# Walking the moving operand and the PSUM output of split matmuls from the last column to the first

## Chip, cores and metric

The kernel runs on one core of one Trainium2 chip. The metric is the device time of one execution in microseconds, as the median of several runs.

## What is computed

The reference is one block of a perceiver with a latent `x` of 256 tokens by 512 features and a context of 25088 tokens by 512 features: a cross attention with a sigmoid in place of the softmax, a causal self attention with compressed keys and values, and a mixture of eight experts with one expert per token. Nearly all of the arithmetic is in the cross attention, which cut to what matters is:

```python
qp = layernorm(x) @ Wq.T + bq            # 256 x 128
kp = ctx @ Wk.T + bk                     # 25088 x 128
vp = ctx @ Wv.T + bv                     # 25088 x 512
z  = sigmoid(qp @ kp.T / sqrt(128))      # 256 x 25088
x  = x + z @ vp
x  = x + attn(layernorm(x))              # causal, 16 heads, rotary part
x  = x + ffn(layernorm(x))               # argmax over 8 experts, relu(g)^2 * u
```

All inputs are fp32.

## The kernel before

An fp32 product is made of three matmuls in a 4-byte format of TensorE that the program calls fp32r. Each operand is split into a high part (the value copied to fp32r) and a low part (the value less its high part). The helper `split` does that: ScalarE copies (line 64), VectorE subtracts (line 65). The helper `mm3` then issues three matmuls into one PSUM tile: high by high (line 68), high by low (line 69), low by high (line 70). `ahi` and `alo` are the stationary operand, loaded into the array ahead of each matmul; `bhi` and `blo` are the moving operand, whose columns are streamed through it; `ps` is the output in PSUM, one column for each moving column.

The value projection is not applied to the context: since `z @ (ctx @ Wv.T)` is `(z @ ctx) @ Wv.T`, the kernel accumulates `z @ ctx` over all keys and applies `Wv` once at the end.

The context is worked off in 49 chunks of 512 keys. It is loaded twice from HBM in two layouts, features first (`rT`) and keys first (`rN`), each 1 MB per chunk, on SyncE's queue, two to three chunks ahead. For one chunk the loop does the following:

- `kp_mm`: four calls of `mm3` over blocks of 128 features, with `wk` stationary and the split `T` moving, 512 columns, into the tile `kp_ps`; `kp_out` adds the bias and splits the result.
- `scores`: twice per chunk, two calls of `mm3` each, with 128 keys of `kp` stationary and `qp` moving, 256 columns, into the two halves of one PSUM bank, the tile `sc`; then the sigmoid (`z`), its sum over keys (`zacc`) and its split.
- `av`: eight calls of `mm3` per chunk, with `z` stationary and the split `N` moving, 512 columns, into `acc`, two PSUM banks that stay open over all chunks.

Besides, `prepare` splits the weights of the experts and of the last projection a piece at a time and spills them to HBM.

After the loop come the value projection (`V`, tile `v_ps`), the self attention, whose matmuls are mostly plain fp32 ones outside `mm3` (the scores `S` at line 428, among others), its output projection (`WO`, tile `wo_ps`), and the experts (`GU`, tile `gu`, 256 columns, and `DN`, tile `fo`, 512 columns). `V`, `WO`, `GU` and `DN` go through `mm3` too, and so does the projection of the queries (`qp_ps`, 256 columns) at the start.

The order on each engine is the order in which the program is written: the function `in_order` ties every instruction of TensorE, ScalarE, VectorE and GpSimd to the one before it on its engine. Waits between engines come from the tiles that they share.

Of the kernel before, what the change touches and what calls it, by code (L numbers as in the profile page):

```python
# [48 lines left out]
def body(ctx, tc, a, out, nch=NCH):  # L49
# [15 lines left out]
        eng.tensor_tensor(lo, src, f(hi), ALU.subtract)  # L65

    def mm3(ps, ahi, alo, bhi, blo, first, last):
        mm(ps, lhsT=ahi, rhs=bhi, start=first, stop=False)  # L68
        mm(ps, lhsT=ahi, rhs=blo, start=False, stop=False)  # L69
        mm(ps, lhsT=alo, rhs=bhi, start=False, stop=last)  # L70
# [4 lines left out]
    def bank(name):  # L75
        return psum.tile([P, D], F32, tag="b", name=name, bufs=6)
# [91 lines left out]
    def kp_mm(c, blocks=range(KD)):  # L168
        th, tl = sT[c]
        if c not in kp:  # L170
            kp[c] = bank(f"kp_ps{c}")
        ps = kp[c]
        for j in blocks:
            mm3(ps, wk[0][:, toks(j)], wk[1][:, toks(j)], th[:, j, :], tl[:, j, :], j == 0, j == KD - 1)
# [6 lines left out]
    def scores(c, p):  # L181
        ps = bank(f"sc{c}_{p}").rearrange("p (i t) -> p i t", i=2)
        for i in range(2):
            t = toks(2 * p + i)
            mm3(ps[:, i, :], kp[c][0][:, t], kp[c][1][:, t], qp[0], qp[1], True, True)
        z = sb.tile([P, 2, T], F32, tag="z", name=f"z{c}_{p}", bufs=2)
        nc.scalar.activation(z, ps, AF.Sigmoid, scale=1.0 / math.sqrt(128.0))  # L187
        zz[c, p] = pair(f"z{c}_{p}", [P, 2, T], "z", 2 * LAG)
        tt2(zacc, zacc, z, ALU.add)  # L189
        split(*zz[c, p], z)  # L190

    def av(c, t, q):
        zh, zl = zz[c, t // 2]
        nh, nl = sN[c]
        mm3(acc[q], zh[:, t % 2, toks(q)], zl[:, t % 2, toks(q)], nh[:, t, :], nl[:, t, :],
            c == 0 and t == 0, c == nch - 1 and t == NT - 1)
# [48 lines left out]
    ps = bank("qp_ps")[:, :T]  # L245
# [319 lines left out]
    ps = bank("rows_ps")  # L565
# [205 lines left out]
```

## Time and profile before

| | us |
|---|---|
| median of 3 runs (lowest to highest) | 586.33 (585.92 to 586.8) |
| the profiled execution's own time | 586.28 |
| its span, first to last instruction | 584.5 |
| TensorE busy | 570.6 |
| VectorE busy | 459.7 |
| ScalarE busy | 395.1 |
| mean granted TensorE clock | 1.0 |

A profile is of one execution. In it, PE is TensorE's matmuls, PEld its loads of the stationary operand, DVE is VectorE, ACT is ScalarE, POOL is GpSimd and SP is SyncE. A line of the groups gives the code line, the engine, the operation, the tiles (output <- inputs), the shape and the count, then the busy time in us and the mean of one instruction in ns, then the idle time of the engine just before. In the 40 slices each digit is a share in tenths. The chain of waits is followed back from the last instruction to whatever released it; in order of time each of its pieces is given with its start, its length and its engine, tile and line. Matmuls are pipelined, and the ends of their records are modelled, so their starts say more than their lengths.

### The profile page before, as it was taken

What the parts mean: (1) busy time and instruction counts of PE and PEld (TensorE: products, weight loads), DVE (VectorE), ACT (ScalarE), POOL (GpSimd) and SP (SyncE); (2) the same over time, 40 slices, a digit from 0 to 9 for tenths busy, and PEclk for the clock granted to TensorE, in tenths of its full rate; (3) what the DMA queues carried; (4) which work ended last, traced back from release to release, by engine and by line L of the source; (5) the groups of instructions that cost most, each with busy time, mean ns of one, the idle gap of its engine ahead of it and who ended that gap; (6) DMA issues with size and microseconds to landing.
All of it is one profiled execution on the core that took longest, in us unless ns stands there. A gap on an engine that the chain in (4) does not pass through costs nothing.

```text
span 584.5 us, 8061 instructions
## 1 busy us (share of the span) xinstructions
PE 570.6 (98%) x3036; PEld 481.7 (82%) x3036; DVE 459.7 (79%) x528; ACT 395.1 (68%) x512; POOL 21.1 (4%) x28
## 2 busy tenths in 40 slices
PE   4999999999999999999999999999999999999997
PEld 3888888888888888888888888888888887876996
DVE  6898888888888888888888888787878765667543
ACT  5877777777777777777777776767676752574211
POOL 5200000000000000000000000000000041000000
PEclk9999999999999999999999999999999999999999
DMA  8897887879888888788988887565657477700000
GB/s 288 334 368 283 278 295 281 321 278 317 287 324 276 325 271 325 266 337 298 332 282 319 274 337 245 208 225 206 234 198 243 149 295 262 316 1 1 1 1 36
DMA packets 33526, 144.94 MB, mean 248 GB/s; under 512 B 4240, under 2 KB 4432, under 8 KB 19792
## 3 DMA queue, kind: packets, MB, share of 16 engines
q1 hardware_dynamic: 33488, 144.44, 69.3%
q8 instruction: 23, 0.38, 0.2%
q14 instruction: 15, 0.12, 0.1%
HBM read 129.22 MB, written 15.20 MB: 247 GB/s over the span
## 4 chain that ended last, share of the span: by engine, by line
PE 95%; DVE 3%; DMA 1%; issue 0%; POOL 0%; ACT 0%; SPq 0%; POOLq 0%
PE acc L68 15%; PE acc L69 15%; PE acc L70 15%; PE kp_ps L70 8%; PE kp_ps L69 8%; PE kp_ps L68 8%; PE sc L70 4%; PE sc L69 4%; PE sc L68 4%; PE s L428 2%; PE gu L68 1%; PE gu L69 1%; PE gu L70 1%; PE pt L445 1%; DMA wq_r<-in_wq 1%; PE pv L456 1%
## 5 line engine op out<-in xcount | busy, mean ns | idle before, releaser
L68 PE MATMUL acc<-N,z 128*128 128x512 f32 x392 | 153.9, 393 | 0.0
L69 PE MATMUL acc<-N,z 128*128 128x512 f32 x392 | 153.7, 392 | 0.0
L65 DVE TENSOR_TENSOR N<-rN,N 128x2048 fp32r<-128x2048 f32 (+1 forms) x53 | 111.6, 2110 | 52.3 <-ACT N L64 52.2
L70 PE MATMUL acc<-N,z 128*128 128x512 f32 x392 | 152.5, 389 | 0.0
L65 DVE TENSOR_TENSOR T<-rT,T 128x2048 fp32r<-128x2048 f32 (+1 forms) x49 | 110.3, 2252 | 15.3 <-ACT T L64 15.3
L187 ACT ACTIVATE z<-sc 128x512 f32<-128x512 f32 x98 | 58.7, 599 | 66.5 <-PE sc L70 66.2
L64 ACT CAST N<-rN 128x2048 fp32r<-128x2048 f32 (+1 forms) x55 | 94.4, 1725 | 6.1
L64 ACT CAST T<-rT 128x2048 fp32r<-128x2048 f32 (+1 forms) x55 | 94.3, 1721 | 0.9 <-DMA rT<-in_ctxT 0.7
L70 PEld LDWEIGHTS acc<-N,z 128*128 128x128 f32 x392 | 73.6, 188 | 16.0
L68 PEld LDWEIGHTS acc<-N,z 128*128 128x128 f32 x392 | 74.0, 189 | 12.3
L69 PEld LDWEIGHTS acc<-N,z 128*128 128x128 f32 x392 | 74.0, 189 | 11.7
L68 PE MATMUL kp_ps<-T,wk 128*128 128x512 f32 x196 | 76.9, 392 | 0.0
L70 PE MATMUL kp_ps<-T,wk 128*128 128x512 f32 x196 | 76.7, 392 | 0.0
L69 PE MATMUL kp_ps<-T,wk 128*128 128x512 f32 x192 | 74.7, 389 | 0.0
L189 DVE TENSOR_TENSOR zacc<-zacc,z 128x512 f32<-128x512 f32 x98 | 67.2, 686 | 3.7 <-ACT z L187 1.7
L65 DVE TENSOR_TENSOR z<-z,z 128x512 fp32r<-128x512 f32 x98 | 67.3, 686 | 0.0
L64 ACT CAST z<-z 128x512 fp32r<-128x512 f32 x98 | 61.0, 623 | 3.1
L178 ACT ACTIVATE kp<-kp_ps,bk 128x512 fp32r<-128x512 f32 x49 | 33.9, 691 | 39.9 <-PE kp_ps L70 39.9
L70 PE MATMUL sc<-qp,kp 128*128 128x256 f32 x196 | 55.8, 285 | 0.1
L69 PE MATMUL sc<-qp,kp 128*128 128x256 f32 x196 | 55.4, 283 | 0.0
L68 PE MATMUL sc<-qp,kp 128*128 128x256 f32 x196 | 54.9, 280 | 0.0
L68 PEld LDWEIGHTS kp_ps<-T,wk 128*128 128x128 f32 x196 | 37.1, 189 | 7.8
(177 smaller groups left out, 658.5 us busy)
## 6 DMA issues: line engine op xcount, KB each, us to landing
rN<-in_ctxN SPq DMA_DIRECT2D x49, 1024.0 KB, 5.7
rT<-in_ctxT SPq DMA_DIRECT2D x47, 1024.0 KB, 5.5
sp_gu<-w_gu SPq DMA_DIRECT2D x32, 256.0 KB, 4.3
gu<-sp_gu SPq DMA_DIRECT2D x8, 1024.0 KB, 6.0
r_gu<-in_gu SPq DMA_DIRECT2D x16, 256.0 KB, 5.7
sp_dn<-w_dn SPq DMA_DIRECT2D x16, 256.0 KB, 4.3
dn<-sp_dn SPq DMA_DIRECT2D x16, 256.0 KB, 6.0
r_dn<-in_dn SPq DMA_DIRECT2D x8, 256.0 KB, 6.1
```

Of the source, the lines that this page charges most:

```text
L64: copy(hi, src)
L65: eng.tensor_tensor(lo, src, f(hi), ALU.subtract)
L68: mm(ps, lhsT=ahi, rhs=bhi, start=first, stop=False)
L69: mm(ps, lhsT=ahi, rhs=blo, start=False, stop=False)
L70: mm(ps, lhsT=alo, rhs=bhi, start=False, stop=last)
L178: nc.scalar.activation(kp[c][0], ps, AF.Identity, bias=bk)
L187: nc.scalar.activation(z, ps, AF.Sigmoid, scale=1.0 / math.sqrt(128.0))
L189: tt2(zacc, zacc, z, ALU.add)
L428: mm(p3[:, h - h0:h - h0 + 2, :], lhsT=qs[:, tt, h // 2, g, :], rhs=kbd[g // 2][:, g % 2, h:h + 2, :nk], start=tt == 1, stop=tt == 0 and h ...
L445: nc.tensor.transpose(ps[:, toks(i * (tt + 1) + kt)], pr[tt, u][:, i, toks(kt)], ident)
L456: mm(pv[tt][r, g, :], lhsT=vs[kt][:, g * P + r.start:g * P + r.stop], rhs=pt[tt, u][:, toks(i * (tt + 1) + kt)], start=kt == 0, stop=kt == tt)
```

## The change

`mm3` reverses the column axis of its PSUM output and of both moving operands ahead of its three matmuls. The column that was streamed first is now streamed last, and is written to the same place in PSUM as before. The stationary operands are left as they are, and so are all matmuls outside `mm3`.

```diff
     def mm3(ps, ahi, alo, bhi, blo, first, last):
+
+        ps, bhi, blo = ps[:, ::-1], bhi[:, ::-1], blo[:, ::-1]
         mm(ps, lhsT=ahi, rhs=bhi, start=first, stop=False)
         mm(ps, lhsT=ahi, rhs=blo, start=False, stop=False)
         mm(ps, lhsT=alo, rhs=bhi, start=False, stop=last)
```

The three matmuls stand on lines 70 to 72 of the changed file, and everything below them two lines further down.

## Prediction

> **What bounds the kernel now.** I read the page's first two parts, then the chain of waits, then the instruction groups.
>
> ```profile
> PE 570.6 (98%) x3036; PEld 481.7 (82%) x3036; DVE 459.7 (79%) x528; ACT 395.1 (68%) x512; POOL 21.1 (4%) x28
> PE   4999999999999999999999999999999999999997
> PEclk9999999999999999999999999999999999999999
> PE 95%; DVE 3%; DMA 1%; issue 0%; POOL 0%; ACT 0%; SPq 0%; POOLq 0%
> ```
>
> The reader is to see that TensorE works in all 40 slices at the full granted clock, and that 95% of the chain that ended last is TensorE. "Busy" alone proves little for a pipelined engine; the chain does, because it stays on the engine and names no wait. The groups say which matmuls:
>
> ```profile
> L68 PE MATMUL acc<-N,z 128*128 128x512 f32 x392 | 153.9, 393 | 0.0
> L68 PE MATMUL kp_ps<-T,wk 128*128 128x512 f32 x196 | 76.9, 392 | 0.0
> L68 PE MATMUL sc<-qp,kp 128*128 128x256 f32 x196 | 54.9, 280 | 0.0
> ```
>
> Lines 68, 69 and 70 are the three matmuls of mm3, and the three tiles have such rows for each. The 392 ns is a record from start to modelled end and overlaps the next. What a matmul costs is the distance to the next start, and the chain, in order of time, gives that:
>
> ```profile
> 298.30 0.23 PE kp_ps L68
> ...
> 303.74 0.12 PE sc L68
> ...
> 304.45 0.23 PE acc L68
> ...
> 305.84 0.12 PE sc L68
> ```
>
> From 298.30 to 303.74 lie 24 matmuls of 512 columns: 227 ns each. From 303.74 to 304.45, six of 256 columns: 118 ns. From 304.45 to 305.84, six of 512: 232 ns; the acc stream mixes 227 and 232, and I take 229. Doubling the columns from 256 to 512 adds 109 ns, so a matmul costs some 0.43 ns a column and about 10 ns fixed. The stage is set by columns.
>
> The same view shows what half that rate looks like, in two places:
>
> ```profile
> 10.68 0.43 PE kp_ps L68
> 11.11 0.43 PE kp_ps L69
> ...
> 13.24 0.21 PE qp_ps L68
> ...
> 521.33 0.86 PE s L428 x2
> ```
>
> The first matmuls of the run, the same instructions as later, take 427 ns (10.68 to 13.24, six) and the first qp ones 213 ns. The plain fp32 matmuls of the scores take 430 ns for 512 columns. In both, the fixed cost is nearly gone beside the doubled column time.
>
> **What the Trainium skill says.** (1) "Advanced Engine Details and Errata", PSUM Cachelines: 8-byte lines, two fp32 values; "Any non-contiguous AP significantly slows down matmuls"; every two consecutive elements should be contiguous. No row before has a step other than one in the innermost dimension, so the trace neither agrees nor disagrees. (2) "SBUF — State Buffer", A bandwidth-pool intuition that's wrong, note on cachelines: 16-byte lines, full bandwidth needs two hits in a line. A walk by minus one has four fp32 hits in each line, and two in each PSUM line: read by the letter this lets the reversed walk go free. (3) "TensorE: Matmul & The Clock Gate", Back-to-back issue gap: N/1.2 ns cold and N/2.4 + 2.5 ns warm. The trace agrees on the first (427 and 213 ns); of the second it shows 227 and 118, about 11 ns over, where the page has 216 and 109. (4) "Advanced Engine Details and Errata", 2x-1p Requirements: VectorE's packed mode takes a step of +1 or -1. That is another engine, a hint only that -1 can count as contiguous.
>
> **The change part by part.** No instruction, DMA, wait or tile is added, removed or moved. The reversed operands cover the same bytes, so each split, each copy out of PSUM and each DMA waits for the same matmul as before; a reader waits for the end of a whole matmul, so that column 0 is now written last makes nobody later. SP's and POOL's queues are not touched. The stationary operand keeps its walk, and so do the matmuls outside mm3 (plain fp32, transposes, masks). Slicing is done while the program is built and costs no device time.
>
> What is left is the rate at which 2652 matmuls stream: acc 1176, kp 588, sc 588, gu 192, qp 12, fo 48, v and wo 24 each, counted in the groups. Nothing before shows a reversed stream, so it is bounded from both sides:
> - At best the walk is free: 0. Slightly better cannot be excluded, because I cannot say what the 11 ns over the page's gap are made of.
> - At worst in the likely class, two consecutive columns no longer merge into one access, and the stream falls to one column where it had two. The price of that is in the rows above: 427 to 430 ns for 512 columns, 213 to 215 for 256. I take 428 and 214.
>
> The sum at half rate:
> - kp: 588 x (428 - 227) = 118 us
> - acc: 1176 x (428 - 229) = 234 us
> - sc: 588 x (214 - 118) = 56 us
> - gu and qp: 204 x 96 = 20 us
> - v, wo, fo: 96 x (428 - 230) = 19 us
>
> Together 447 us. The twelve matmuls at the start of the run that already go at 427 and 213 ns come off (6 x 0.20 + 6 x 0.10 = 1.8 us). TensorE idles 13.9 us in all (584.5 - 570.6), most of it before its first matmul and around the last copies, which a longer stream cannot fill; I take off 2 us more for the gaps that it can. That leaves 443 us, all on the path: TensorE is the bound and becomes more so. VectorE's 459.7 us and ScalarE's 395.1 us of work would fall to 45% and 38% of the span, and their waits for sc and kp would grow without costing anything; the DMA, 0.85 busy in the windows of the main loop, would fall to about half that.
>
> The profiled execution took 586.28 us with a span of 584.5, so 1.8 us lie around the span; the median of the runs, 586.33, is the same within 0.05. The half-rate case gives 584.5 + 443 + 1.8 = 1029 us.
>
> I choose half rate as the likeliest, over free: the skill's sentence on PSUM names a direct slowdown of matmuls, the merging of two fp32 columns into one 8-byte line has to hold on the write side and on the moving side at once, and either failing is enough. [...]
>
> **The rivals.**
> - **The walk is free** (also if the build folds the two reversals away: reversing both sides permutes columns and leaves each product where it was, so nothing of the work depends on it). For it: two consecutive columns stay in one line whichever way they are walked, and both ends are aligned, since each slice starts at a multiple of 256 columns. Against it: the skill's "any". Time: 586 us, change 0.
> - **A fixed price per matmul.** The stream keeps its rate but its start or its turn at the end costs some cycles more. Each nanosecond on 2652 matmuls is 2.7 us; 1 to 10 ns give 589 to 613 us. Nothing in the profile speaks for it except that a fixed cost of about 11 ns exists.
> - **Faster.** That fixed cost belongs to the warm three-pass matmul: bf16 mask matmuls of 512 columns start the next after 0.21 us in the timeline (504.93 to 505.14) where these take 227 ns. If it comes from the order in which a matmul's first columns meet what the one before left in flight, the reversed order could remove it: 2652 x 10.5 ns = 28 us, giving 558 us. It decides from 0.45 ns a matmul (1.2 us in all). Against it: all three passes are reversed together, so consecutive matmuls meet each other as before, end against start.
> - **Worse than half rate.** One element at a time on both sides with no overlap, or a fall to a quarter: some 850 ns for 512 columns and 425 for 256. On 1860 and 792 matmuls that adds 1860 x 0.62 + 792 x 0.31 = 1399 us: about 1980 us. Only the word "significantly" speaks for it.
>
> **How the numbers follow.** A measurement of this kernel can tell about 0.2%, 1.2 us, from no change. Half rate: 0.50, 1029 us. Its own range is 1015 to 1066: the low end if the waits in the prologue and tail absorb 14 us, the high end if the fixed cost of 11 to 13 ns stays on top of the doubled columns (2652 x 0.012 = 32 us, with a little for the spread of the acc starts). Free: 0.20. A fixed price per matmul: 0.12. Worse than half rate: 0.06. Faster: 0.12. Slower is then 0.50 + 0.12 + 0.06 = 0.68, within the bound 0.20, faster 0.12. Cases of more than one sign hold real chance, so the range that holds 8 in 10 runs from the free case (585) to the top of half rate (1066); it leaves out the faster case and the quarter rate, 0.18. The middle of that range is nearly empty: it is wide because the price of a reversed stream is unknown before, in one step.
>
> **What would show it right or wrong.** Right: in the chain of the changed kernel kp_ps and acc pieces of 0.43 us and sc pieces of 0.21 us where there were 0.23 and 0.12, the granted clock still 1.0, TensorE's share of the chain at 97% or more, VectorE near 45% and ScalarE near 38% busy, with the same number and length of their instructions; the L428 pieces, which mm3 does not touch, still 0.86 for two. The first six kp_ps matmuls of the run would stay at 0.43: if these too double, the rate is lost per array cycle, and the loss is more than the merging of two columns. Free would show 0.23 and 0.12 everywhere. A fixed price would show the same nanoseconds added at 256 and at 512 columns. What makes the prediction wrong in kind is a matmul that keeps its start-to-start of 227 ns; what makes it wrong in size is a doubled one off 428.

## The result, and the profile after

| | before | changed |
|---|---|---|
| median, us | 586.57 (585.92 to 587.5, 4 runs) | 595.04 (594.31 to 595.31, 4 runs) |
| profiled execution: its time, its span | 586.28, 584.5 | 595.31, 593.5 |

The changed kernel is slower by 8.5 us: ratio 1.0141, 95% interval 1.0124 to 1.0159. The sign was forecast; the size, 1029 us, was not.

The page of the changed kernel, its busy times, TensorE's two rows of slices, and the chain by engine:

```profile
PE 580.0 (98%) x3036; PEld 481.8 (81%) x3036; DVE 459.7 (77%) x528; ACT 394.1 (66%) x512; POOL 21.1 (4%) x28
PE   4999999999999999999999999999999998999997
PEclk9999999999999999999999999999999999999999
PE 97%; DVE 1%; POOL 1%; DMA 0%; issue 0%; ACT 0%; POOLq 0%
```

TensorE was the bound and still is, at the same granted clock. VectorE's work is the same to 0.1 us. The groups of mm3, one row for each tile:

```profile
L70 PE MATMUL acc<-N,z 128*128 128x512 f32 x392 | 155.7, 397 | 0.0
L70 PE MATMUL kp_ps<-T,wk 128*128 128x512 f32 x196 | 78.5, 400 | 0.0
L70 PE MATMUL sc<-qp,kp 128*128 128x256 f32 x196 | 55.3, 282 | 0.0
```

The mean records at 512 columns are 4 to 8 ns longer than before (393 and 392), those at 256 columns 2 ns (280). The chain in order of time, one chunk of the loop. A piece of a matmul starts there where the record before it ends, some 160 ns after the matmul's own start; over a whole run of equal matmuls the distance from piece to piece is that from start to start:

```profile
303.50 0.23 PE kp_ps L70
...
306.30 0.23 PE acc L70
...
309.10 0.12 PE sc L70
...
309.81 0.23 PE acc L70
...
311.21 0.12 PE sc L70
```

The pieces are printed as 0.23 and 0.12 as before; only distances over several of them show the change. Twelve kp matmuls take 2.80 us, 233 ns each, where they took 227; twelve of acc likewise 2.80 us. Six of sc take 0.71 us, 118 ns, as before. The six of acc behind them take 1.40 us, 233 ns each, where they took 232.

Means over all starts between 40 and 440 us of the two traces: kp 226.7 to 233.3 ns, acc 228.9 to 233.3, sc 118.8 to 118.9. The sum closes: 588 x 6.6 ns = 3.9 us and 1176 x 4.4 ns = 5.2 us make 9.1 us. The stretch from the first kp matmul to the last of acc grew from 482.3 to 491.5 us, by 9.2; the rest of the span is 0.3 us shorter at the start and within 0.1 us behind the loop. So the change is a longer start-to-start distance of the 512-column matmuls of the loop, 2 to 3% of it. It is no chance collision with other engines or with DMA: matmul by matmul, the distances of some 40 like chunks agree within 1 ns in each of the two kernels.

The two places that I had named as a sign:

```profile
10.37 0.43 PE kp_ps L70
...
12.93 0.21 PE qp_ps L70
...
531.20 0.86 PE s L430 x2
```

At the start of the run the reversed matmuls still take 427 ns (10.37 to 12.93, six): no price is seen there. The matmuls outside mm3 keep their 430 ns.

### The profile page after: what moved, and what is told of

It is laid out like the page before. It is cut to its first block, busy times and chain, and to the rows that moved or that the text cites. A ratio compares the mean times of both kernels' runs of the same rounds, so it can differ in the third digit from the quotient of the medians.

```text
span 593.5 us, 8111 instructions
## 1 busy us (share of the span) xinstructions
PE 580.0 (98%) x3036; PEld 481.8 (81%) x3036; DVE 459.7 (77%) x528; ACT 394.1 (66%) x512; POOL 21.1 (4%) x28
## 4 chain that ended last, share of the span: by engine, by line
PE 97%; DVE 1%; POOL 1%; DMA 0%; issue 0%; ACT 0%; POOLq 0%
PE acc L71 15%; PE acc L70 15%; PE acc L72 15%; PE kp_ps L71 8%; PE kp_ps L70 8%; PE kp_ps L72 8%; PE sc L72 4%; PE sc L71 4%; PE sc L70 4%; PE s L430 2%; PE gu L70 1%; PE gu L72 1%; PE gu L71 1%; PE q_ps L356 1%; PE pt L447 1%; PE pv L458 1%
## 5 line engine op out<-in xcount | busy, mean ns | idle before, releaser
L71 PE MATMUL acc<-N,z 128*128 128x512 f32 x392 | 156.0, 398 | 0.0
L70 PE MATMUL acc<-N,z 128*128 128x512 f32 x392 | 155.7, 397 | 0.0
L72 PE MATMUL acc<-N,z 128*128 128x512 f32 x392 | 155.5, 397 | 0.0
L71 PEld LDWEIGHTS acc<-N,z 128*128 128x128 f32 x392 | 73.7, 188 | 13.3
L70 PE MATMUL kp_ps<-T,wk 128*128 128x512 f32 x196 | 78.5, 400 | 0.0
L72 PE MATMUL kp_ps<-T,wk 128*128 128x512 f32 x196 | 78.3, 400 | 0.0
L71 PE MATMUL kp_ps<-T,wk 128*128 128x512 f32 x192 | 76.3, 397 | 0.0
```

## The experiments

Four questions: which side pays, which property of the walk, how it goes with length and with the neighbouring matmuls, and whether any use of it is a gain. Where an edit is said to be for 512 columns only, it stands under `if ps.shape[-1] == 512`.

### Which side pays

```diff
 def mm3(ps, ahi, alo, bhi, blo, first, last):
+    bhi, blo = bhi[:, ::-1], blo[:, ::-1]
```

> Only the moving operands of mm3 are reversed; the PSUM outputs are walked forward, so every mm3 product has its columns in reversed order (the work is the same, the values are not the reference's). In the changed kernel every mm3 matmul of 512 columns starts the next after 233 ns instead of 227 (kp and the first half of acc) or 231 (the second half of acc), while those of 256 columns stay at 118 to 119 ns. Theory A, the price sits on the read of the moving operand: 233 ns here too, about 595 us (+8.5 us). Theory B, it sits on the write to PSUM: 227 ns and 586.5 us, no change. Theory C, each side pays half: about 230 ns, 590 to 591 us.

Measured: 595.44 us, ratio 1.0158 (1.0142 to 1.0174).

```diff
 def mm3(ps, ahi, alo, bhi, blo, first, last):
+    ps = ps[:, ::-1]
```

> Only the PSUM outputs of mm3 are reversed; the moving operands are walked forward (again the columns of every mm3 product stand in reversed order). Theory A, read of the moving operand: 227 ns for 512 columns of kp, 586.5 us. Theory B, write to PSUM: 233 ns, about 595 us. Theory C, half each: 230 ns, 590 to 591 us. If both this and the run with the moving operand alone give 233 ns, the two prices run side by side and are not added.

Measured: 586.05 us, ratio 0.9998 (0.999 to 1.0007). The chain in order of time of the first, then of the second:

```profile
303.80 0.23 PE kp_ps L69
...
306.60 0.23 PE acc L69
```

```profile
306.86 0.23 PE kp_ps L69
...
309.58 0.23 PE acc L69
```

Twelve kp matmuls take 2.80 us with the moving operand reversed and 2.72 us with the output reversed: 233 against 227 ns. Theory A holds. The read of the moving operand pays all of it; a PSUM output written from the last column to the first is free, in accumulating matmuls too. With one side reversed alone, the build cannot have folded the reversal away, since the columns land in another order.

### Which matmuls pay

```diff
+    if ps.shape[-1] == 512:
+        ps, bhi, blo = ps[:, ::-1], bhi[:, ::-1], blo[:, ::-1]
```

> Both sides reversed, but only in the mm3 matmuls of 512 columns (kp, acc, v, wo, fo: 1860 of 2652). If the 256-column matmuls hide the price behind the load of their weights (their 118 ns is that load's pace, not the columns'), all of the change is here: 595 us, with 233 ns for kp and acc. If the price is on every matmul and the 256-column ones pay it too, about 592 us (8.5 us less 792 of 2652).

Measured: 595.7 us, ratio 1.0165 (1.0146 to 1.0184), kp at 233.3 ns and acc at 233.7. All of the change is in the 512-column matmuls.

```diff
+    if ps.shape[-1] == 256:
+        ps, bhi, blo = ps[:, ::-1], bhi[:, ::-1], blo[:, ::-1]
```

> Both sides reversed only in the mm3 matmuls of 256 columns (sc, gu, qp: 792 of 2652). Hidden behind the weight load: 586.5 us within 0.5, sc at 118.8 ns in the mean. A fixed price on every matmul: 792 x 6.7 ns = 5.3 us more, 592 us. If instead the second half of acc, which follows sc and runs at 231 ns before, is set by the state that sc leaves the pipe in, acc's times there may move although its own walk is forward.

Measured: 584.07 us, ratio 0.9967 (0.9956 to 0.9979): no price, but a gain of 2.1 us. It is taken up again below.

### Which property of the walk

Four walks that cover the same columns, on both sides, for 512 columns only. `t` is each of ps, bhi and blo.

```diff
+    t.rearrange("p (a b) -> p a b", b=4)[:, :, ::-1]     # inner4
```

> 512-column mm3 only: the columns are walked in groups of four fp32 (16 bytes) from the first group to the last, but inside each group from the last to the first, on moving operand and output alike. Theory order inside a line: the price comes from taking a group's elements backwards, 233 ns or more. Theory descending addresses: groups ascend here, so 227 ns and 586 us. If a walk with two steps costs by itself, both this and the next run are above 233 ns.

Measured: 585.88 us, ratio 0.9999 (0.9989 to 1.0009), kp at 226.7 ns.

```diff
+    t.rearrange("p (a b) -> p a b", b=4)[:, ::-1, :]     # lines4
```

> 512-column mm3 only: groups of four fp32 walked from the last group to the first, inside each group forward. Theory descending addresses, or the start at the far end of the row: 233 ns, about 595 us. Theory order inside a line: 227 ns, 586 us.

Measured: 595.93 us, ratio 1.0171 (1.0132 to 1.0211), kp at 233.3 ns.

```diff
+    t.rearrange("p (a b) -> p a b", b=256)[:, ::-1, :]   # halves
```

> 512-column mm3 only: columns 256 to 511 are walked first and then 0 to 255, each half forward, on both sides. Theory start at the far part of the row: 233 ns, 595 us. Theory descending addresses: only one backward jump, 227 ns, 586 us.

Measured: 585.75 us, ratio 0.999 (0.998 to 1.0), kp at 226.7 ns.

```diff
+    t.rearrange("p (a b) -> p a b", b=256)[:, :, ::-1]   # halves_rev
```

> 512-column mm3 only: columns 255 to 0 and then 511 to 256, each half reversed. Theory start at the far end of the row: it starts in the middle, 227 ns, 586 us. Theory descending addresses: 233 ns, 595 us.

Measured: 595.53 us, ratio 1.0159 (1.0125 to 1.0193), kp at 233.3 ns.

The four answers agree on one thing. Backwards inside each 16 bytes is free, and so is one backward jump over half the row, to a start in the middle. What costs is that the groups of 16 bytes follow one another downwards, wherever the walk begins. A negative step as such, or a pattern of two steps, costs nothing. The free walks were not folded into the plain one: the instruction records of the traces carry the moving operand as 4 by 128 elements in inner4 and lines4, and as 256 by 2 in halves and halves_rev. They do not carry the sign of a step. No group other than 4 and 256 columns was run, so that 16 bytes is the unit that counts is not shown: a descent in larger groups may cost as well. The chain in order of time of lines4 and of inner4, kp:

```profile
303.26 0.23 PE kp_ps L70
...
306.06 0.23 PE acc L70
```

```profile
307.25 0.23 PE kp_ps L70
...
309.97 0.23 PE acc L70
```

2.80 against 2.72 us for twelve.

### How it goes with length

The expectations below reckon with bare 213.3 ns for 512 columns, 0.4167 ns a column. That is an estimate: half of the 426.7 ns that the first matmuls of the run take. The 226.7 ns of a steady run are then 13.3 ns more.

```diff
+    n = ps.shape[-1]
+    if n == 512:                      # reversed partner; forward: [:, :320]
+        p3, h3, l3 = ps[:, 319::-1], bhi[:, 319::-1], blo[:, 319::-1]
+        ps, bhi = ps[:, ::-1], bhi[:, ::-1]
...                                     # other lengths: p3, h3, l3 = ps, bhi, blo
     mm(ps, lhsT=ahi, rhs=bhi, start=first, stop=False)
-    mm(ps, lhsT=ahi, rhs=blo, start=False, stop=False)
-    mm(ps, lhsT=alo, rhs=bhi, start=False, stop=last)
+    mm(p3, lhsT=ahi, rhs=l3, start=False, stop=False)
+    mm(p3, lhsT=alo, rhs=h3, start=False, stop=last)
```

> The partner of the next run: everything walks forward, but the second and third pass of every 512-column mm3 stream only the first 320 columns (the low parts of the last 192 columns are left out of the result). These matmuls should cost 227 - 192 x 0.4167 = 147 ns from start to start, if the cost over the bare columns is fixed at 13.3 ns. 1860 x 2/3 = 1240 matmuls lose 80 ns each: about 487 us.

> The same with moving operand and output reversed in every matmul of the 512-column mm3 calls, the short ones too (the same columns are left out). Fixed price for each matmul: the short ones take 6.7 ns more than those of the forward partner. A price on each column, which 512 columns show as 6.7 ns: 320 show 4.2 ns more. The long first pass shows 6.7 in both cases. In time 1860 x 6.7 = 12 us (fixed) against 1240 x 4.2 + 620 x 6.7 = 9.4 us (each column) above the partner, less what the forward partner loses after the score matmuls.

Measured: 555.17 and 556.88 us, far from the 487 us of the expectation, because TensorE, at 89% and 90% busy, was no longer the only bound. The distances still tell. In steady runs the three passes start the next after 231, 147 and 149 ns forward, and after 233, 147 and 147 reversed: 527 ns each way. Both forms of price that were expected (6.7 or 4.2 ns on the short passes) are missed, and so is the 6.7 ns on the long pass, which shows 2. Between shorter matmuls the whole price is gone, so it does not hang on a matmul's own length alone.

```diff
+    ps, bhi, blo = (t[:, :n or 512][:, ::-1] for t in (ps, bhi, blo))   # forward: without [::-1]
...
+    n = 504 in kp blocks 1 to 3, 448 in acc key tiles 0 and 1 (from the second chunk on)
```

> Forward partner of the next run. In kp, blocks 1 to 3 stream only 504 columns, and in acc the first two of four key tiles only 448 (the last columns are left out of the result there), in all three passes, so that runs of equal length stand behind one another. 227, 233, 120 and 147 ns, seen so far in steady runs, are 34, 35, 18 and 22 times 6.67 ns. Theory step: a matmul starts on a grid of 6.67 ns, and a small delay counts as a whole step or not at all; then 448 columns (186.7 + 13.3) take 200 ns = 30 steps, and 504 (210 + 13.3 = 223.3) go up to 227 or alternate. Theory smooth: 504 take 223.3 ns.

> The same lengths with both sides of the 512-column mm3 calls reversed (so the walk starts at column 503 or 447 where it is cut). Theory fixed: 448 columns take 206.7 ns and 504 some 230. Theory each column: 448 take 205.8 and 504 take 229.9; that is hardly apart, so the run before with 320 columns, which took no more than forward in its short passes, counts here: a price that starts only beyond some length shows as 0 at 448 and 6.7 at 512. Theory step: 200 or 206.7, and 226.7 or 233.3, nothing between in a steady run.

Measured: 572.79 and 578.89 us. With `n` of 384 in kp and 320 in acc:

> Forward partner of the next run: kp blocks 1 to 3 stream 384 columns, and acc key tiles 0 and 1 stream 320 (the last columns are left out of the result there). With the 13.3 ns of 512 columns on top, 384 take 173.3 ns and 320 take 146.7.

> The same lengths reversed. A price for each matmul whatever its length: some 4 to 7 ns more than forward at 384 and at 320. A price that only long walks pay: the same as forward at 320, and 0 to 4 ns more at 384. A price in proportion to the columns, from 6.7 at 512: 5.0 and 4.2 ns.

Measured: 565.84 and 568.18 us, TensorE 91% and 92% busy. The mean distance of the starts between 40 and 440 us, in ns. The cut runs are short, nine matmuls in kp and twelve in acc, and begin with a transient. So the last column has the price once the run is settled: the last three or six matmuls of kp, the last ten of acc.

| columns | forward | reversed | price, mean | price, settled |
|---|---|---|---|---|
| 512 (kp) | 226.7 | 233.3 | 6.6 | 6.6 |
| 504 (kp) | 226.9 | 228.9 | 2.0 | 2.2 |
| 448 (acc) | 202.6 | 206.7 | 4.1 | 4.0 |
| 384 (kp) | 176.2 | 177.8 | 1.6 | 4.5 |
| 320 (acc) | 146.0 | 146.7 | 0.7 | 0.0 |
| 256 (sc) | 118.8 | 118.9 | 0.1 | not reached in six |

At 384 the two columns differ most. Forward, the three blocks take 0.52, 0.54 and 0.52 us in the mean; only the last one, at 173.3 ns a matmul, is steady as far as three matmuls can show it, and that is the forecast to the tenth. The last three of a run, forward and then reversed (177.8 ns), in the timeline, which gives a matmul's own start:

```profile
305.74 0.33 PE L70 MATMUL kp_ps<-T,wk 128*128 128x384 f32 x1
...
306.26 0.31 PE L70 MATMUL acc<-N,z 128*128 128x320 f32 x1
```

```profile
307.23 0.34 PE L70 MATMUL kp_ps<-T,wk 128*128 128x384 f32 x1
...
307.76 0.31 PE L70 MATMUL acc<-N,z 128*128 128x320 f32 x1
```

The price is neither one amount for each matmul nor in proportion to the columns: it is nothing at 320 and uneven beyond. Part of the unevenness is in the forward walk: 504 columns take as long as 512 there. The step of 6.67 ns that I had supposed is refuted as a law for single matmuls, since 448 columns settle neither on 200 nor on 206.7 forward, and 504 reversed run steadily at 229.

### Neighbours: the stationary load, and one pass of three

```diff
+    if ps.shape[-1] == 512:                         # reversed partner alone
+        ps, bhi, blo = (t[:, ::-1] for t in (ps, bhi, blo))
+    ps, ahi, alo = ps[:m], ahi[:, :m], alo[:, :m]   # m = 64 in kp blocks 1, 2 and (from the second chunk on) acc key tiles 0, 1
```

> Forward partner of the next run: in kp blocks 1 and 2 and in acc key tiles 0 and 1 the stationary operand has 64 columns instead of 128 (the upper 64 output rows of these products are left out)[...]; the moving side is as before. If the 13.3 ns over the bare 213.3 come from the load of the next stationary operand beside the stream, these matmuls go below 227 ns, to about 220; if not, they stay at 227.

> The same with both sides of the 512-column mm3 calls reversed (the same rows left out). Theory moving read by itself: the matmuls with 64 stationary columns take 6.7 ns more than their forward partners, as those with 128 do. Theory load of the stationary operand: their price falls to about half, 3.3 ns, or to nothing, while those with 128 columns stay at 233.

Measured: 588.53 us forward, ratio 1.004 (1.0025 to 1.0055), and 595.84 us reversed, ratio 1.0164 (1.0145 to 1.0184). Half the columns shorten the load's record, though not to half, and make the forward stream slower, not faster. Two groups of the loads of half_fwd, of 64 and of 128 columns:

```profile
L71 PEld LDWEIGHTS kp_ps<-T,wk 128*64 128x64 f32 x98 | 13.2, 135 | 6.4
L71 PEld LDWEIGHTS kp_ps<-T,wk 128*128 128x128 f32 x98 | 18.5, 189 | 7.5 <-ACT T L64 0.6
```

The timeline of half_fwd, from the first of six kp matmuls with 64 columns to the one behind them:

```profile
290.11 0.40 PE L71 MATMUL kp_ps<-T,wk 128*64 128x512 f32 x1
...
291.49 0.39 PE L71 MATMUL kp_ps<-T,wk 128*128 128x512 f32 x1
```

Six take 1.38 us; in the mean over all chunks they go 236, 229, 224, 226, 234, 231 ns, 230.1 each, where they went 227. The reversed stream stays at 233.3. So a shorter load removes neither the 13 ns nor, in level, the 233. The price as a difference is 3.2 ns at 64 columns. That is the figure which the load theory forecast (3.3), but it came from a slower forward stream and not, as the theory meant it, from a faster reversed one; the other theory forecast 6.7 and missed. Whether the load has a part in the price is left open by this pair.

```diff
-    mm(ps, lhsT=ahi, rhs=blo, start=False, stop=False)
+    p2, l2 = (t[:, ::-1] if t.shape[-1] == 512 else t for t in (ps, blo))
+    mm(p2, lhsT=ahi, rhs=l2, start=False, stop=False)
```

> Only the second pass (high by low) of each 512-column mm3 is reversed, on both sides. Each reversed matmul pays for itself: in a steady run of kp three starts take 227 + 227 + 233 ns, and of the 9.5 us that all three passes cost a third is left, about 589.5 us. A state of the stream that needs several reversed matmuls in a row: 586.5 us. A price at each change of direction: two changes in three matmuls, 13 ns in three, 593 us or more.

Measured: 588.79 us, ratio 1.0048 (1.0031 to 1.0064), 2.5 us where a third of 8.5 to 9.5 is 2.8 to 3.2. A steady run of kp goes 226.7, 232.5, 227.5 ns: 6.7 ns more in three, where three reversed passes pay 20. The reversed pass pays, its neighbours next to nothing, and a change of direction adds nothing to that.

### The version that beats both

The edit of cols256 again: both sides reversed in the 256-column matmuls alone.

> The 256-column mm3 matmuls alone reversed on both sides, for a narrower interval: 584.1 us against 586.2, ratio 0.9965. By the trace of the first such run, six sc matmuls and the six of acc behind them take 707 + 1373 ns where before they take 713 + 1387, 20 ns less, 98 times: 2 us. If that was chance, the ratio holds 1.

Measured: 584.61 us against 586.25, ratio 0.9968 (0.9954 to 0.9981). The gain stands, at 0.3%. Its chain in order of time, around one pair of score matmuls, and the same stretch of the kernel before (from the prediction's view: 303.74, 304.45, 305.84):

```profile
312.63 0.12 PE sc L70
...
313.33 0.23 PE acc L70
...
314.71 0.12 PE sc L70
```

Six sc and six acc take 2.08 us here, 2.10 before. In the trace's starts, sc falls from 118.8 to 117.9 ns in the mean, and the acc matmuls that follow, which walk forward in both kernels, from 233, 236, 228, 233, 231, 226 to 235, 231, 227, 226, 227, 227: the slow stretch behind the scores ends after two matmuls instead of five. 20 ns, 98 times, are 2.0 us; the two runs gave 2.1 and 1.6. Why the stream recovers sooner was not settled, nor was one side of the 256-column matmuls reversed alone. In out_only, where their output is reversed, the distances behind the scores are the old ones (233, 236, 229, 232, 231, 227), which points to the moving read here too.

## Why the prediction was wrong

- **The bound, and what the change touches: right.** The work of the other engines is as before, their busy times within 1 us; the distance between the matmuls of mm3 is the one thing that changed. TensorE's chain share rose to 97%, which I had named as a sign, but it was met without half rate. The other signs of half rate failed: the pieces stayed at 0.23 and 0.12 us, and VectorE and ScalarE at 77% and 66% busy instead of 45% and 38%.
- **Size: the step that failed is "I take 428 and 214".** The term should have been 233 and 119. It came out of choosing the half-rate class at 0.50, and that choice leaned on the sentence "Any non-contiguous AP significantly slows down matmuls" (the Trainium skill, "Advanced Engine Details and Errata", PSUM Cachelines). The measurement decides: reversed PSUM output, 0.9998. The page's other sentence, that every two consecutive elements should be contiguous, is met by a reversed walk. The skill's note on 16-byte lines in "SBUF — State Buffer" (it stands under "Door 1: The DMA port swizzle", not where the prediction puts it), which I had read as letting the walk go free, came nearer: the order inside 16 bytes is free (inner4), and only a descent from group to group has a price.
- **"Either failing is enough": the step before it was wrong.** Neither side fell to half rate: the output costs nothing, the moving read 6.6 ns of 227. I had two memories with one unknown each and let the word "any" price both, and I put the 8-byte line, which the page gives for PSUM, on the moving side as well, though the moving operands, the tiles `T`, `N` and `qp`, lie in SBUF.
- **Rows that could not carry the price.** The 427 and 430 ns were read from matmuls at the start of the run and from another format. They show what half rate would cost, and nothing in them links it to the direction of a walk.
- **The chain's starts.** I read the starts of the chain's pieces as starts of matmuls. A piece starts where the record before it ends. This did no harm: in the loop the distances over the runs that I used are the same, and at the start of the run five distances from start to start are 427 ns as well.
- **The rival that came nearest** is the fixed price per matmul, 1 to 10 ns, 589 to 613 us, at 0.12. The mean over 2652 matmuls is 8.5 us / 2652 = 3.2 ns. It held in size, not in form: 512 columns pay 6.6 ns in kp and 4.4 in acc, 256 and 320 next to nothing, so "the same nanoseconds added at 256 and at 512 columns" failed. The 11 ns that it started from compare the stream with a formula which the page, as cited in (3) of the prediction, gives for a single matmul on its own; no run shows them to be a cost of their own. That its range holds 595 is luck. So it is with the whole range, 585 to 1066 us: it holds 595 only because it reaches from the free walk to half rate.
- **The faster rival** failed for this kernel. A gain shows only where the 256-column matmuls alone are reversed, and whether it comes about as the rival had it was not shown. The argument against it, that matmuls meet each other as before, treated every start-to-start distance as a property of the matmul alone. But the 232 ns behind the scores, which I had averaged away ("the acc stream mixes 227 and 232, and I take 229"), come only after the 256-column matmuls. A shorter slow stretch there gives 15 of the 20 ns that the best version gains for each six scores, and the slow stretch is also why acc pays 4.4 ns and not 6.6: half of its matmuls had already been slow.
- **The first matmuls of the run: right, but for no reason that the runs bear out.** They stay at 427 ns. I expected that because they already went at half rate. As it turned out, the 6.6 ns of the steady run are not added to the slow one; why was not tested.

What stays open: what in the read of a descending row costs time, why it goes so unevenly with length and with the neighbours, how large a group must be for its descent to be free, and whether the load of the next stationary operand, which runs beside it, has a part in it. Reversing the stationary operand to test this was not tried, nor was a moving operand of another format.

## What to carry to other kernels

Price an access pattern one side at a time and one property at a time (sign of the step, order inside a line, order of lines, start), and do not let a general sentence on contiguity stand for a factor of two when the nearest rows cannot show it. In a kernel whose chain is a stream of matmuls, 4 to 7 ns on each long one is 1.5% of the time. Such a price does not show in the pieces of the chain, printed as 0.23 us in both kernels; it shows in distances over a dozen of them. Leave the first matmuls after a change of length out of such a mean, or give them apart: at 384 columns they turned a price of 4.5 ns into 1.6. Where long and short matmuls alternate, look at the first few after each change of length: there the stream ran slower than in its steady state here, and the walk that is bad for long matmuls helped when the short ones took it.

## What was not expected of the hardware

- The direction of the moving read matters and that of the PSUM write does not: 233.3 against 226.7 ns at 512 columns, for the same bytes.
- A row of 504 columns forward takes as long as one of 512: 226.7 ns each in a settled run.
- Reversed matmuls of 512 columns that alternate with two of 320 cost nothing: 527 ns for the three in either direction.
- Matmuls with 64 stationary columns stream more slowly than with 128, 230.1 against 226.7 ns, though the record of their load is 54 ns shorter.
- Behind a run of six 256-column matmuls, five 512-column ones in a row are slower, by 1 to 9 ns (228 to 236 against 227).
